# Audio tower on one core: the second normalisation's block turns moved ahead of two expert tiles, bo's third addition moved, gate products on 317 columns

## The chip, the core and the metric

The kernel runs on one core of a Trainium2 chip. The core has five engines with queues of their own: TensorE (PE, with its weight loads shown as PEld), VectorE (DVE), ScalarE (ACT), GpSimd (POOL) and SyncE (SP), which here only issues DMAs. Each engine executes its instructions in the order in which the program gives them, and waits on semaphores for the others. The metric is the device time of one execution in microseconds (us); lower is better.

## What is computed

A batch of 64 signals of 80000 samples is cut into 157 frames of 512 samples each. A DCT of the frames is the embedding `h`. Then follow one attention-like layer and one mixture-of-experts layer, each on a normalised input and added to `h`. The reference, cut to what matters:

```python
h = einsum('bfh,kh->bfk', frames, D)                  # 64 x 157 x 512

x = layernorm(h)                                      # attention
key, qry = exp(1j*pi*tanh(x@Wk+bk)), exp(1j*pi*tanh(x@Wq+bq))
V = x @ Wv + bv
total = sum over 4 sets s of w[s] * Re( cumsum(key_s * V) * conj(qry_s) )
gate = sigmoid(x @ Wg + bg)
total = gate*total + (1-gate)*sigmoid(pos_weight)*retrieved_pos
h = h + x + (total / norm) @ Wo + bo

x = layernorm(h)                                      # experts
scores = softmax(mean(x, axis=1) @ Wg2 + bg2)         # one expert of 16 for each signal
idx = argmax(scores)
h = h + max(scores) * (x @ We[idx] + be[idx])
```

All data is float32.

## The kernel before

**Tiles.** Signals are worked on in 16 groups of 4 (`g` = 0 to 15). A group's tokens lie in five tiles of 128: tiles 0 to 3 hold 32 tokens of each of the 4 signals, and the tail tile (`TAIL`) holds the last 29 of each, filled up to 32. Where the tokens are columns (`xT`, `gT`), the order of the tiles is 0, 1, TAIL, 2, 3, and the 640 columns are two halves of `HN` = 320: the first half is tile 0, tile 1 and signals 0 and 1 of the tail, the second half is signals 2 and 3 of the tail and tiles 2 and 3. So the last 3 columns of the first half (`Q - LT` = 32 - 29) belong to no token.

**Products by seven.** The three large products of a group (values, gate, output) are each done as a 2 x 2 block product with seven block products instead of eight. `product` (line 445) does one for values and output, `gate_product` (line 655) for the gate. Some of their operands are sums of blocks, made by `token_sums`: `new(0)`, `new(2)` on the engine it is given, then `new(1)` and `new(3)` on DVE (line 99), one at each `next(made)`. `new(1)` is used by product 6, `new(3)` by product 3, the last one. `gather` adds a product from PSUM into the results. In the gate, products 4 and 7 take the second half of the columns, products 1, 2, 3, 5 and 6 the first half or sums over both halves, and all have 320 columns. PSUM holds four tiles of two banks (`psum()`), taken in turn by whatever TensorE computes next.

**Stages of a group.** The whole schedule is written by hand: in the order of the program each engine gets its queue. For g from 1 to 15:

1. `project_and_values(g)`: the projection to phases (TensorE, line 600; tanh on ACT), then the value products and the value of the tail. Between them stands work for the second normalisation of the group before: `turn_blocks(g - 1, n)` turns 32 x 32 blocks of the normalised tile n on DVE (line 785) into `blocks2`; `normal2(g - 1, 0)` and `normal2(g - 1, 1)` normalise tiles 0 and 1 on ACT (line 776). When all five tiles are turned, `move_blocks` sends them as 16 DMAs, ten from SP's queue and six from POOL's, to `x2T`, and `xsum`, `route_own`, `route_all` (a small matmul, line 840) and `pick` choose the experts; `fetch` has their weights brought by four indirect DMAs from POOL (4 MB). `keep_value` and `keep_product` (which calls `gather`) bring values from PSUM to SBUF.
2. `gate(g)`: the seven gate products, and between them the scores (line 681), `pick_gate`, `bias` (an indirect DMA for be) and the embedding of group g + 1 with its statistics.
3. `experts_and_embedding(g)`: the expert tiles TAIL, 0 and 1 of group g - 1, and for group g + 1 the normalisation of the residual (`embed_res`, ACT, line 323).
4. `attention(g)`: `add_bo` (POOL, line 327) adds bo to the residual tiles of group g + 1. `read(g, c)` for c = 0 to 3 is the reading of the attention (TensorE, line 697); its result is multiplied into `gT` by DVE (line 704), and a second part added by POOL for c = 0 and 1 (line 708, from a copy `rest` that ACT makes, line 707), by DVE for c = 2 and 3. Then come the seven output products in the order 1, 2, 6, 7, 5, 4, 3, with `statistics2` (means and deviations of the second normalisation, DVE lines 232 and 233, then POOL lines 237 to 244) for TAIL after the first and for tiles 2 and 3 at product 4. After the products come the expert tiles 2 and 3 of group g - 1, the statistics of tiles 0 and 1, `value_sums(g + 1)` (the first two token sums of the next group's values, on POOL), and `normal2` of tiles 2 and 3.

**What stands in whose queue.** `expert(g, n)` is 32 matmuls (64 records in the trace for two tiles), then `expert_out`: DVE multiplies the PSUM tile by the gate and adds it to the residual (line 956), and four DMAs store the tile, from SP. In the program of before, DVE's statistics of tiles 0 and 1 stand behind the two outputs of expert tiles 2 and 3, the five turns behind these, some of them behind the second sum of the values. `blocks2` lies in the same buffer as `gT`, one after the other, and the normalised tiles `x2` in the buffers of the values `v`.

Lines that the change and the prediction's steps touch: 392 `alike`, 399 `token_sums`, 455 `gather`, 647 `gate_product`, 1090 `project_and_values`, 1173 `value_sums`, 1180 `attention`.

Of the kernel before, what the change touches and what calls it, by code (L numbers as in the profile page):

```python
# [28 lines left out]
Q = P // GB  # L29
NM = LP // Q  # L30
TAIL = NM - 1
SLOT = [0, 1, 3, 4, 2]
HT = P // 2
HN = HT + 2 * P
LT = L - Q * TAIL
# [18 lines left out]
def audio_tower(ctx: ExitStack, tc: tile.TileContext, a, out):  # L54
# [21 lines left out]
    nc = tc.nc  # L76
# [14 lines left out]
    def psum():  # L91

        return ps_mm.tile([P, 2, 512], F32, tag="mm", name="mm")
# [6 lines left out]
    add = lambda *x: nc.vector.tensor_tensor(*x, ALU.add)  # L100
# [287 lines left out]
    def halves(x):  # L388

        return [[half(x, m)[:, 2 * k : 2 * k + 2] for k in range(2)] for m in range(2)]  # L390

    def alike(first, second):

        n = 2 * P
        yield first[:, :, :n], second[:, :, -n:]
        if first.shape[2] > n:
            yield first[:, :, n:], second[:, :, :-n]

    def token_sums(g, tail=True, engine=nc.vector):

# [20 lines left out]
    def operand(g, i):  # L421

        (a11, a12), (a21, a22) = S[g]["blocks"]
        return {1: a11, 2: a12, 4: a22}[i] if i in (1, 2, 4) else S[g]["sums"][{3: 3, 5: 0, 6: 1, 7: 2}[i]]
# [3 lines left out]
    def room(g, i):  # L428

        held = S[g].setdefault("held", {})  # L430
        first = i not in ONTO
        ps = psum() if first else held.pop(ONTO[i])
        if i in ONTO.values():
            held[i] = ps
        return ps, first
# [19 lines left out]
    def gather(i, ps, c):  # L455

        (c11, c12), (c21, c22) = c  # L460
        if i == 1:
            nc.scalar.copy(c12, ps)
        elif i == 2:
            nc.scalar.copy(c11, ps)  # L464
        elif i in (4, 7):
            for (x, y), (_, to) in zip(alike(c12, ps), alike(c12, c21 if i == 4 else c22)):
                add(to, x, y)
        elif i == 5:
            for x, to in alike(ps, c22):
                add(to, x, to)  # L470
        else:
            add(c12, ps, c12)


    def value_buffer(g, n):
# [113 lines left out]
    def by_halves(ps):  # L589

        return ps[:, :, :HN]
# [18 lines left out]
    def fold_phases(g):  # L610
        u = S[g]["u"]
        nc.vector.scalar_tensor_tensor(u[:, 1], u[:, 0], -1.0, u[:, 0], ALU.mult, ALU.max)
# [34 lines left out]
    def gate_product(g, i):  # L647

        s = S[g]
        if i == 1:  # L650
            s["gT"] = p1.tile([P, C, 2 * HN], F32, tag="gT", name="gT")
        (ps, first), rhs, w = room(g, i), operand(g, i), fac_g[i]
        for o in range(2):
            for c in range(2):
                nc.tensor.matmul(  # L655
                    ps[:, o, :HN],
                    w[:, c, o * P : (o + 1) * P],
                    rhs[:, c],
                    start=(first and c == 0),
                    stop=(c == 1),  # L660
                    skip_group_check=not first,
                )
        part = halves(s["gT"])
        if i != 2:
            gather(i, by_halves(ps), part)
        for k, m, n in ((2, 0, 0), (5, 1, 1), (3, 0, 1), (4, 1, 0)):
            if k == i:
                for o in range(2):
                    to = part[m][n][:, o]
                    c = 2 * n + o  # L670
                    of = ps[:, o, :HN] if i == 2 else to
                    nc.scalar.activation(to, of, AF.Tanh, bias=hbg[:, c : c + 1], scale=0.5)  # L672

    def scores(g):
# [85 lines left out]
    def at_end(g, n):  # L760

        return g + 1 == NG and n in (3, 0, 1)

    def normal2(g, n):
        s = S[g]
        if n == TAIL:
            x = p1.tile([P, D], F32, tag="v_t", name="x2_t")
        else:
            if n % 2 == 0:
                s["x22"] = p1.tile([P, 2, D], F32, tag="v", name="x2", bufs=2)  # L770
            x = s["x22"][:, n % 2, :]
        rstd, shift = s.pop(("st2", n))
        if at_end(g, n):
            nc.vector.tensor_scalar(x, s["res"][n], shift, rstd, ALU.subtract, ALU.mult)
        else:
            nc.scalar.activation(x, s["res"][n], AF.Identity, bias=shift, scale=rstd)  # L776
        s["x2", n] = x

    def turn_blocks(g, n):

        s = S[g]
        if n == TAIL:
            s["blocks2"] = p1.tile([P, C * GB, LP], F32, tag="gT", name="turned2")
        to = s["blocks2"].rearrange("p (q c) t -> p c q t", c=C)[..., Q * n : Q * (n + 1)]
        nc.vector.transpose(to, s.pop(("x2", n)).rearrange("p (c q t) -> p c q t", c=C, q=GB))
# [155 lines left out]
    def expert_chunk(g, n, c, ps):  # L941

        s = S[g]
        for i in range(GB):
            nc.tensor.matmul(  # L945
                ps[Q * i : Q * (i + 1), :],
                s["x2T"][:, c, i, Q * n : Q * (n + 1)],
                s["ws"][i][:, c, :],
                start=(c == 0),
                stop=(c == C - 1),  # L950
            )
# [13 lines left out]
    def expert(g, n, between=lambda c: None):  # L965
        ps = psum()
        for c in range(C):
            between(c)
            expert_chunk(g, n, c, ps[:, 0, :])
        between(C)  # L970
        expert_out(g, n, ps[:, 0, :])
# [118 lines left out]
    def project_and_values(g):  # L1090

        project(g)
        made = S[g].pop("made")
        turn_blocks(g - 1, TAIL)
        turn_blocks(g - 1, 2)
        fold_phases(g)
        turn_blocks(g - 1, 3)
        value_product(g, 1)
        keep_product(g)
        normal2(g - 1, 0)  # L1100
        normal2(g - 1, 1)
        value(g, TAIL)
        next(made)
        if g == 1:
            for n in (2, 3, TAIL):
                add_bo(g, n)
        turn_blocks(g - 1, 0)
        keep_value(g, TAIL)
        turn_blocks(g - 1, 1)
        moves = move_blocks(g - 1)  # L1110
        next(moves)
        S[g - 1]["late"] = xsum(g - 1, 2 * Q, L)
        value_product(g, 2)
        keep_product(g)
        add_bv(g, 0, slice(0, H))
        next(moves)
        phasors(g)
        value_product(g, 6)
        keep_product(g)
        route(g - 1)  # L1120
        value_product(g, 7)
        keep_product(g)
        route_own(g - 1)
        value_product(g, 5)
        keep_product(g)
        next(made)
        fold_once(g + 1, 0)
        value_product(g, 4)
        keep_product(g)
        route_all(g - 1)  # L1130
        pick(g - 1)
        fetch(g - 1)
        value_product(g, 3)
        keep_product(g)
        weigh()
        fold_twice(g + 1, 0)
# [36 lines left out]
    def value_sums(g):  # L1173

        S[g]["blocks"] = halves(S[g]["xT"])
        S[g]["made"] = made = token_sums(g, engine=nc.gpsimd)
        next(made)
        next(made)

    def attention(g):  # L1180
        ahead = g + 1 < NG
        if ahead and g > 0:
            for n in (0, 1):
                add_bo(g + 1, n)
        if g == 0:
            for _ in weight_sums(wg, t_g, nc.gpsimd):
                pass
        for c in range(C):
            read(g, c)
            if ahead and g > 0:  # L1190
                for n in ((2,), (3, TAIL), (), ())[c]:
                    add_bo(g + 1, n)
        S[g]["blocks"] = halves(S[g]["gT"])
        made = token_sums(g, tail=False)
        if g == 0:
            for n in (0, 1):
                add_bo(1, n)
        for i in (1, 2, 6, 7, 5, 4, 3):
            output_product(g, i)
            if i == 1:  # L1200
                for _ in range(4 if g else 3):
                    next(made)
                if g == 0:
                    scale_all(1)
                output_tail(g)
                statistics2(g, (TAIL,))
            elif i == 6:
                normal2(g, TAIL)
            elif i == 7 and g == 0:
                next(made)  # L1210
            elif i == 5 and g == 0:
                value_sums(1)
            elif i == 5 and ahead:
                scale_all(g + 1)
        if 0 < g and ahead:
            expert(g - 1, 2)
            expert(g - 1, 3)
        for of in ((0, 1),) if ahead else ((0,), (1,)):
            statistics2(g, of)
        if 0 < g and ahead:  # L1220
            value_sums(g + 1)
        normal2(g, 2)
        normal2(g, 3)
        if not ahead:
            normal2(g, 0)

    for g in range(NG):
        if g == 0:
# [12 lines left out]
    g = NG - 1  # L1241
# [158 lines left out]
```

## Time and profile before

| | us |
|---|---|
| median of 3 runs | 1310.64 (1310.27 to 1313.44) |
| the profiled execution | 1311.08 |
| its span, first to last instruction | 1309.1 |
| start to the first projection (group 0) | 45.8 |
| group 0 | 49.1 |
| groups 1 and 2 | 79.2 and 79.3 |
| groups 3 to 14 together | 952.3 (79.36 each) |
| group 15 and the end | 103.4 |

A group is counted here from the first matmul of its projection (line 600) to that of the next. One of the middle groups, from 412.15 to 491.50, has this busy time of the engines by stage, in us:

| stage | from:to | length | PE | DVE | ACT | POOL |
|---|---|---|---|---|---|---|
| projection and values | 412.15:430.45 | 18.30 | 18.30 | 16.37 | 8.61 | 10.88 |
| gate and embedding | 430.45:451.25 | 20.80 | 20.80 | 16.37 | 8.52 | 10.50 |
| experts TAIL, 0, 1 | 451.25:461.68 | 10.43 | 10.43 | 9.05 | 3.24 | 4.62 |
| reading | 461.68:468.81 | 7.13 | 7.13 | 4.10 | 3.50 | 5.68 |
| output products | 468.81:484.61 | 15.80 | 15.80 | 14.07 | 1.40 | 4.18 |
| experts 2, 3 | 484.61:491.50 | 6.89 | 6.89 | 3.71 | 1.52 | 1.43 |

A float32 matmul leaves two records in the trace. A record's length is from its start to its modelled end, and records overlap, so that the distance of two starts, not the length, is what a matmul takes of TensorE. Where a matmul or a weight load waits, the wait lies before its start, or within the record if the weights come late.

### The profile page before, as it was taken

The page shows a single profiled execution, that of the slowest core. Times are in us where ns is not written, and L with a number is a line of the kernel's source. Part 1 is how long each engine was busy: PE and PEld are TensorE (multiplying, and loading weights), DVE is VectorE, ACT ScalarE, POOL GpSimd, SP SyncE. Part 2 cuts the span into 40 slices and gives each one's busy share as a digit, 9 for nine tenths or more (in the row PEclk, how much of TensorE's full clock was granted, in tenths as well). Part 3 has the DMA queues.
Part 4 walks back from the last instruction along what each step waited for, and adds up shares of the span by engine and source line. Part 5 has one row for each costly group of instructions (what it writes and reads, how often), then busy time and mean ns, then how long its engine had stood idle before and what let it go on. Part 6 is the DMA issues. An engine that isn't in the chain of part 4 may idle for free.

```text
span 1309.1 us, 25859 instructions
## 1 busy us (share of the span) xinstructions
PE 1302.9 (100%) x10040; PEld 863.6 (66%) x10040; DVE 1026.9 (78%) x2056; ACT 432.5 (33%) x768; POOL 603.1 (46%) x766
## 2 busy tenths in 40 slices
PE   9999999999999999999999999999999999999998
PEld 6677666676666667666676666766666676666762
DVE  5888787788878878788787877888778787877673
ACT  2524334142432324334143331424323243341410
POOL 2356445344553446435364453446434364343424
PEclk9999999999999999999999999999999999999999
DMA  7015224152341425324252241523314252241506
GB/s 240 1 52 177 75 61 184 41 177 75 111 151 34 168 79 169 95 57 147 82 178 75 68 179 38 178 75 123 135 45 161 82 178 83 57 151 37 179 9 209
DMA packets 60578, 144.45 MB, mean 110 GB/s; under 512 B 14136, under 2 KB 31432, under 8 KB 52520
## 3 DMA queue, kind: packets, MB, share of 16 engines
q1 hardware_dynamic: 45620, 62.68, 16.9%
q0 software_dynamic: 14336, 79.47, 16.7%
q8 instruction: 80, 1.31, 0.4%
q10 hardware_dynamic: 500, 0.64, 0.2%
q14 instruction: 42, 0.34, 0.1%
HBM read 102.47 MB, written 20.62 MB: 94 GB/s over the span
## 4 chain that ended last, share of the span: by engine, by line
PE 98%; POOL 1%; DMA 1%; issue 0%; DVE 0%; POOLq 0%
PE mm L445 29%; PE mm L945 20%; PE mm L655 18%; PE mm L250 9%; PE mm L697 9%; PE mm L270 3%; PE mm L272 3%; PE mm L600 3%; PE mm L636 1%; PE mm L681 1%; PE mm L201 1%; DMA t_v<-in_we,rows 1%; PE mm L219 0%; PE mm L191 0%; PE mm L840 0%
## 5 line engine op out<-in xcount | busy, mean ns | idle before, releaser
L945 PE MATMUL mm<-we,x2T 128*32 128x512 f32 x2400 | 264.1, 593 | 0.0
L945 PEld LDWEIGHTS mm<-we,x2T 128*32 128x32 f32 x2400 | 74.8, 110 | 167.3 <-issue 165.5
L237 POOL TENSOR_SCALAR rstd<-mv 128x2 f32<-128x2 f32 (+1 forms) x50 | 11.8, 236 | 292.6 <-DVE mv L233 292.5
L697 PE MATMUL mm<-att,v 32*128 32x320 f32 (+3 forms) x2048 | 113.1, 357 | 0.0
L697 PEld LDWEIGHTS mm<-att,v 32*128 32x128 f32 x2048 | 94.5, 185 | 22.1 <-issue 12.6
L956 DVE SCALAR_TENSOR_TENSOR res<-mm,gate,res 128x512 f32<-128x512 f32 x64 | 47.9, 749 | 73.1 <-PE mm L945 73.1
L237 POOL TENSOR_SCALAR dev<-mv 128x5 f32<-128x5 f32 (+1 forms) x20 | 10.5, 525 | 196.8 <-DVE mv L233 196.2
L776 ACT ACTIVATE x<-res,shift,rstd 128x512 f32<-128x512 f32 x61 | 46.4, 806 | 162.6 <-POOL shift L244 161.4
L704 DVE TENSOR_TENSOR gT<-mm,gT 128x320 f32<-128x320 f32 x128 | 59.5, 484 | 42.6 <-PE mm L697 42.5
L100 DVE TENSOR_TENSOR gT<-mm,gT 128x320 f32<-128x320 f32 (+3 forms) x128 | 71.4, 567 | 23.9 <-PE mm L655 20.9
L232 DVE BATCH_NORM_STATS2 st<-res 128x6 f32<-128x512 f32 x128 | 87.7, 685 | 2.8
L327 POOL TENSOR_TENSOR res<-res,bo 128x512 f32<-128x512 f32 x64 | 81.6, 1288 | 13.1 <-ACT res L323 13.0
L445 PE MATMUL mm<-t_o,sum 128*128 128x256 f32 x384 | 85.5, 379 | 0.0
L515 POOL TENSOR_TENSOR v<-v,bv 128x512 f32<-128x512 f32 (+1 forms) x45 | 72.7, 1635 | 24.5 <-ACT v L464 24.4
L672 ACT ACTIVATE gT<-gT,hbg 128x320 f32<-128x320 f32 x90 | 45.6, 554 | 112.8 <-DVE gT L100 112.8
L323 ACT ACTIVATE res<-res,shift,more 128x512 f32<-128x512 f32 x64 | 46.9, 803 | 103.7 <-POOL more L313 103.7
L445 PE MATMUL mm<-t_v,sum 128*128 128x256 f32 x360 | 80.1, 379 | 0.0
L445 PEld LDWEIGHTS mm<-t_o,sum 128*128 128x128 f32 x384 | 73.0, 190 | 9.9
L899 POOL DMA_INDIRECT we<-in_we,rows x60 | 60.4, 1006 | 34.3 <-DVE rows L895 20.3
L445 PEld LDWEIGHTS mm<-t_v,sum 128*128 128x128 f32 x360 | 68.4, 190 | 9.3
L250 PE MATMUL mm<-wv,xT 128*128 128x512 f32 x160 | 71.8, 592 | 0.0
L655 PE MATMUL mm<-xT,wg 128*128 128x320 f32 x240 | 69.5, 432 | 0.0
(220 smaller groups left out, 2877.9 us busy)
## 6 DMA issues: line engine op xcount, KB each, us to landing
xT<-in_frames SPq DMA_DIRECT2D x32, 640.0 KB
out<-res SPq DMA_DIRECT2D x236, 64.0 KB
x2T<-turned SPq DMA_DIRECT2D x150, 80.0 KB
x2T<-turned POOLq DMA_DIRECT2D x90, 80.0 KB
scale<-row SPq DMA_DIRECT2D x15, 320.0 KB
out<-res_t SPq DMA_DIRECT2D x62, 32.0 KB
out<-res_t SPq DMA_DIRECT2D x62, 26.0 KB
wg<-in_wg SPq DMA_DIRECT2D x1, 1024.0 KB
```

The source lines that it names most:

```text
L100: add = lambda *x: nc.vector.tensor_tensor(*x, ALU.add)
L232: nc.vector.bn_stats(st, h)
L250: nc.tensor.matmul(ps, tile_of(x[:, c], n), w[:, c, :], start=(c == 0), stop=(c == C - 1))
L327: nc.gpsimd.tensor_tensor(r, r, bo, ALU.add)
L445: nc.tensor.matmul(ps[:, b, :], lhs[:, c, P * b : P * (b + 1)], w[:, c, :], start=(first and c == 0), stop=(c == 1), skip_group_check=not ...
L515: nc.gpsimd.tensor_tensor(v, v, by, ALU.add)
L655: nc.tensor.matmul(ps[:, o, :HN], w[:, c, o * P : (o + 1) * P], rhs[:, c], start=(first and c == 0), stop=(c == 1), skip_group_check=not f ...
L697: nc.tensor.matmul(to, s["v", n][q, c * P : (c + 1) * P], by, start=(n == 3), stop=(n == TAIL))
L704: nc.vector.tensor_tensor(th, r[:, :, 0], th, ALU.mult)
L899: nc.gpsimd.indirect_dma_start(out=ws[b][:, n * k : n * (k + 1)], out_offset=None, in_=of, in_offset=bass.IndirectOffsetOnAxis(ap=rows[:, ...
L945: nc.tensor.matmul(ps[Q * i : Q * (i + 1), :], s["x2T"][:, c, i, Q * n : Q * (n + 1)], s["ws"][i][:, c, :], start=(c == 0), stop=(c == C - 1),
L956: nc.vector.scalar_tensor_tensor(o, ps, s["gate"], o, ALU.mult, ALU.add)
```

## The change

1. **Gate products on 317 columns.** Products 1, 2, 3, 5 and 6 of the gate run over 317 columns instead of 320, and the results that they alone make are read and written on 317 columns. Since products 4 and 7 still read all 320 columns of one result, its last 3 columns are set to zero by a memset on POOL when the tile is made.
2. **End of `attention(g)` for g = 1 to 14.** The expert tiles 2 and 3 of group g - 1 go behind the statistics of tiles 0 and 1, the normalisations of tiles 2, 3, 0 and 1, `value_sums(g + 1)` and the turns of TAIL, 2 and 3. The turns of tiles 0 and 1 stand between the two expert tiles. On TensorE nothing changes its place.
3. **`project_and_values(g)` for g = 2 to 15.** The turns and normalisations of the group before are no longer there. The second `next(made)`, the sum `new(3)`, goes from behind `keep_product` of product 5 to before `keep_value` of the tail.
4. **bo.** For g = 1 to 14 `add_bo` of tile 2 stands before the reading and not behind `read(g, 0)`.

For g = 1 the first stage is left as it was.

```diff
@@ gather @@
+        tight = lambda x: x[:, :, : ps.shape[2]]
         if i == 1:
-            nc.scalar.copy(c12, ps)
+            nc.scalar.copy(tight(c12), ps)
...
         else:
-            add(c12, ps, c12)
+            add(tight(c12), ps, tight(c12))
@@ gate_product @@
         if i == 1:
             s["gT"] = p1.tile([P, C, 2 * HN], F32, tag="gT", name="gT")
+            nc.gpsimd.memset(s["gT"][:, :, HN - (Q - LT) : HN], 0.0)
         (ps, first), rhs, w = room(g, i), operand(g, i), fac_g[i]
+        width = HN if i in (4, 7) else HN - (Q - LT)
         for o in range(2):
             for c in range(2):
                 nc.tensor.matmul(
-                    ps[:, o, :HN],
+                    ps[:, o, :width],
                     w[:, c, o * P : (o + 1) * P],
-                    rhs[:, c],
+                    rhs[:, c, :width],
...
@@ project_and_values @@
         project(g)
         made = S[g].pop("made")
-        turn_blocks(g - 1, TAIL)
-        turn_blocks(g - 1, 2)
+        if g == 1:
+            turn_blocks(0, TAIL)
+            turn_blocks(0, 2)
         fold_phases(g)
-        turn_blocks(g - 1, 3)
+        if g == 1:
+            turn_blocks(0, 3)
         value_product(g, 1)
         keep_product(g)
-        normal2(g - 1, 0)
-        normal2(g - 1, 1)
+        if g == 1:
+            normal2(0, 0)
+            normal2(0, 1)
         value(g, TAIL)
         next(made)
         if g == 1:
             for n in (2, 3, TAIL):
                 add_bo(g, n)
-        turn_blocks(g - 1, 0)
+            turn_blocks(0, 0)
+        else:
+            next(made)
         keep_value(g, TAIL)
-        turn_blocks(g - 1, 1)
+        if g == 1:
+            turn_blocks(0, 1)
         moves = move_blocks(g - 1)
...
         value_product(g, 5)
         keep_product(g)
-        next(made)
+        if g == 1:
+            next(made)
@@ attention @@
         if ahead and g > 0:
-            for n in (0, 1):
+            for n in (0, 1, 2):
                 add_bo(g + 1, n)
...
             read(g, c)
             if ahead and g > 0:
-                for n in ((2,), (3, TAIL), (), ())[c]:
+                for n in ((), (3, TAIL), (), ())[c]:
                     add_bo(g + 1, n)
...
-        if 0 < g and ahead:
-            expert(g - 1, 2)
-            expert(g - 1, 3)
         for of in ((0, 1),) if ahead else ((0,), (1,)):
             statistics2(g, of)
-        if 0 < g and ahead:
-            value_sums(g + 1)
         normal2(g, 2)
         normal2(g, 3)
         if not ahead:
             normal2(g, 0)
+        elif g > 0:
+            normal2(g, 0)
+            normal2(g, 1)
+            value_sums(g + 1)
+            for n in (TAIL, 2, 3):
+                turn_blocks(g, n)
+            expert(g - 1, 2)
+            for n in (0, 1):
+                turn_blocks(g, n)
+            expert(g - 1, 3)
```

`alike`, which pairs the columns of two halves, gets an end for its last piece that also holds where the two differ in width.

More of the change, by code (lines that the diff above doesn't have):

```diff
@@ L396, in alike @@
         if first.shape[2] > n:
-            yield first[:, :, n:], second[:, :, :-n]
+            yield first[:, :, n:], second[:, :, : first.shape[2] - n]
     def token_sums(g, tail=True, engine=nc.vector):
@@ L664, in gate_product @@
         if i != 2:
-            gather(i, by_halves(ps), part)
+            gather(i, ps[:, :, :width], part)
         for k, m, n in ((2, 0, 0), (5, 1, 1), (3, 0, 1), (4, 1, 0)):
@@ L670, in gate_product @@
                     c = 2 * n + o
-                    of = ps[:, o, :HN] if i == 2 else to
+                    to = to[:, :width] if m == 0 else to
+                    of = ps[:, o, :width] if i == 2 else to
                     nc.scalar.activation(to, of, AF.Tanh, bias=hbg[:, c : c + 1], scale=0.5)
```

## The prediction

> **What bounds the kernel now.** I read the busy shares and the chain of waits first. Columns of part 1: engine, busy us, share of the span, instructions.
>
> ```profile
> span 1309.1 us, 25859 instructions
> PE 1302.9 (100%) x10040; PEld 863.6 (66%) x10040; DVE 1026.9 (78%) x2056; ACT 432.5 (33%) x768; POOL 603.1 (46%) x766
> ...
> PE 98%; POOL 1%; DMA 1%; issue 0%; DVE 0%; POOLq 0%
> ```
>
> TensorE is busy for all but 6.2 us and is 98% of the chain. So work moved between DVE, ACT and POOL is worth only the TensorE waits that go with it. The busy share hides short waits, because a matmul that waits for its weights counts as busy. I looked for them in the starts on the timeline. A middle group repeats exactly: the projection (L600) starts at 412.15 and at 491.50, 79.35 us apart. In that period I found two places where TensorE waits for something that the change touches. The first, on the timeline (start, length, engine, line, count):
>
> ```profile
> 427.15 0.68 DVE L100 TENSOR_TENSOR v<-mm,v 128x512 f32<-128x512 f32 x1
> 427.75 0.81 DVE L99 TENSOR_TENSOR sum<-xT,sum 128x640 f32<-128x640 f32 x1
> ...
> 428.10 0.41 PEld L840 LDWEIGHTS mm<-own,mean 128*128 128x128 f32 x2
> 428.32 0.33 PE L840 MATMUL mm<-own,mean 128*128 128x64 f32 x2
> ...
> 428.62 0.51 PEld L445 LDWEIGHTS mm<-wv,sum 128*128 128x128 f32 x3
> 428.62 0.70 PE L445 MATMUL mm<-wv,sum 128*128 128x256 f32 x2
> ```
>
> DVE ends the fourth sum (L99) at 428.56, and the weights of value product 3, which are that sum, load at 428.62. TensorE stood for it. The two first matmuls cover 0.70 us where two undisturbed ones (216 ns apart, 379 ns long) cover 0.60: 0.10 us of the wait sits inside a busy record. The second place is at the start of the output products; the last bracket is idle time and its releaser:
>
> ```profile
> 466.35 1.28 POOL L327 TENSOR_TENSOR res<-res,bo 128x512 f32<-128x512 f32 x1
> ...
> 467.58 1.70 POOL L708 TENSOR_TENSOR gT<-gT,rest 128x320 f32<-128x320 f32 x2
> ...
> 469.33 1.16 PEld L445 LDWEIGHTS mm<-wo,gT 128*128 128x128 f32 x6 [0.22 <-POOL gT L708]
> ...
> PEld mm L445 <- POOL gT L708: 3.2, 14, 0.2
> ```
>
> POOL's third bo addition delays its two gT additions of c = 1 to 469.28, and output product 1 needs them. The last line, from the list of waits, says that this happens in 14 groups. Last, the place into which most is moved, around the two expert tiles (64 matmul records from 405.26):
>
> ```profile
> 407.67 0.66 DVE L100 TENSOR_TENSOR res<-mm,res 128x512 f32<-128x512 f32 x1
> ...
> 408.97 0.75 DVE L956 SCALAR_TENSOR_TENSOR res<-mm,gate,res 128x512 f32<-128x512 f32 x1 [0.65 <-PE mm L945]
> ...
> 412.41 0.75 DVE L956 SCALAR_TENSOR_TENSOR res<-mm,gate,res 128x512 f32<-128x512 f32 x1 [2.68 <-PE mm L945]
> ```
>
> DVE idles 3.3 us here for the tiles' outputs, with the statistics queued behind.
>
> **What the Trainium skill says.** "TensorE: Matmul & The Clock Gate", LDWEIGHTS: a load takes its columns over 1.2 GHz, an estimate of 107 ns for 128; two loads that nothing hides stand 0.11 us apart here (428.62 and 428.73), which agrees. The same page, Back-to-back issue gap: N/2.4 + 2.5 ns. The trace differs in the slope: eight 320-column records go from 430.45 to 432.61, 270 ns each, so 0.83 ns per column and record, with two records per float32 matmul. "GPSIMD Engine Reference", Specifications: GpSimd shares VectorE's SBUF interfaces and contends with instructions that have two SBUF inputs. It agrees: the second sum (L99) takes 1.88 us beside POOL's, the fourth, with the same shape, 0.81 us.
>
> **Gate without filling columns.** Five of the seven gate products lose 3 of 320 columns: 5 x 4 matmuls x 2 records x 3 x 0.83 ns = 0.10 us, in 15 groups 1.5 us, all on TensorE. If odd widths are rounded up inside it is 0. DVE and ACT save less than 1% of operations that nobody waits for. The small memset of gT on POOL stands between the expert fetches and be's fetch (437.28). POOL's first memsets show its price: 0.10 us for 128x5. It waits for the last readers of the old tile in that buffer, the block moves, and the DMA share is 0 from 430 on. Behind it be's fetch, a fold and the bv additions run until 443.3, and POOL's next work begins at 455.87. If that cover were gone it would be 0.10 x 15 = 1.5 us; I take 0.
>
> **The fourth sum.** In groups 2 to 15 it moves from behind value product 5 to ahead of keeping the tail value, so it ends near 418 and not at 428.56. Product 3 then waits only for keeping product 5 (427.15 + 0.68 = 427.83), which is before it is its turn. Gain: the loads then follow the one at 428.32 by 0.11 us, to 428.43, so product 3 has weights at 428.54 instead of 428.73: 0.19 us. At most the whole 0.19 + 0.10 us. If another wait is hidden behind it, 0. Taken: 14 x 0.19 = 2.6 us (0 to 4.1).
>
> **bo's third addition.** POOL has done two bo additions by 463.27. A third ends by 464.5, before the first rest is there (464.64), so c = 0 is not delayed. It leaves the place at 466.35, and the c = 1 additions run when their input is ready (466.44) and end near 468.2, before the product's first weights load (468.81). The load at 469.33 is then prefetched; the interval before the next matmul falls from 305 to 216 ns: 14 x 0.09 = 1.2 us. If the first load too was waiting in part (its transition costs 0.05 us more than the others') it is 1.9; if c = 0 were delayed, 0.
>
> **Statistics, normalisations, turns.** Nothing is added: groups 2 to 15 execute the same two statistics, four normalisations and five turns earlier. From 408.33 DVE does the statistics in 1.7 us (their length now), to 410.0; then three turns (0.6 to 0.7 each), to about 412.0, whose last input ACT has at 411.05. The first expert output then ends at 412.8 and not 409.7. POOL needs 1.9 us for the shift (414.85 to 416.71 now), so 412.0; ACT normalises tiles 0 and 1 by 413.6; their turns end at about 414.3; the second output at 415.1 instead of 413.2. Queued behind are SP's stores of the two tiles, 3.1 and 1.9 us later, whose buffers are wanted only in the next gate stage, and the two PSUM tiles. Of four, the first is next taken by the tail value (416.25), the second by value product 6 (421.41): 3.4 and 6.3 us spare. POOL's two sums run from 412.0 to about 416.0 instead of 416.68 to 420.57; DVE's second sum ends by 417.4 even at 1.88 us, wanted at 421.41. Then SP's ten block moves go at 415 instead of 422; POOL's six stay where they are, behind bv, which waits for value product 2. The fetch follows by about 1 us at most; its traffic ends before 448 now and is used at 451.25. All this is off the path: 0. What it does for the path is to leave DVE 3 to 5 us less to do in the value products, cover for the fourth sum.
>
> **Sum.** 1.5 + 2.6 + 1.2 = 5.3 us, with ends of 0 and 7.5. The profiled execution took 1311.08 us (span 1309.1, 2.0 around it): 1305.8. It lies 0.44 above the median shown, 1310.64, so that the median becomes 1305.3. What is late next in a group are the fixed pauses of about 0.1 us where TensorE changes its tile shape; these stay.
>
> **Rivals.**
> Only the columns and bo: product 3's wait is taken over by the next link (keeping product 5 or the route's own matmul). For it: DVE has no gap between 418.38 and 428. Against: 3 to 5 us of its work leave just that stretch, and keeping product 5 ends 0.5 us before it is wanted. Gain 2.7: 1307.9.
> The change doesn't do what it says: the columns are rounded, c = 0 of the reading is held up by the third addition and loses what c = 1 gains. The margin at 464.64 is only 0.1 us. Gain below 1: 1310.
> Slower: a PSUM tile stays taken. The first expert output now stands behind turns that wait for ACT, which waits for POOL's shift. Should that chain or POOL's sums beside DVE's turns hold it beyond 416.25, TensorE stops at the tail value in 14 groups. It decides from 3.4 us of delay on; 1 us beyond it costs 14, less 5.3: 1319.3. Against: turns beside POOL's sums take 0.70 us now, as without.
>
> **Numbers.** Forecast 0.70, only columns and bo 0.14, nothing moves 0.07, slower 0.09. A measurement of this kernel can tell 0.3%, 3.9 us, from no change: faster needs 1306.7 or less. The forecast's own range (gains of 4 to 7.5, 1303.1 to 1306.7) lies just beyond it. I put faster at 0.70, same at 0.21, slower at 0.09. The range takes in the second case: 1303.3 to 1308.8.
>
> **What would show it.** Right: a period near 79.0 us in groups 2 to 14; the load of product 3's weights 0.11 us behind the route's; no wait of PEld for POOL gT; gate records at 267 ns for five products; expert outputs near 412 and 414.5. Wrong: any gap on TensorE at the tail value or product 6, a wait of ACT for the memset at gate product 1, or bo's additions ending after the first rest.

## The result and the profile after

The changed kernel takes 1305.9 us, median of 6 runs (1304.4 to 1307.56), beside 1311.57 us for the kernel before, median of 6 runs (1310.27 to 1313.44). The ratio is 0.996, with a 95% interval of 0.9949 to 0.997: faster by 0.43%, 5.7 us. The prediction was 1305.3 us.

The page of the changed kernel, its span, busy times and chain of waits:

```profile
span 1302.5 us, 25848 instructions
PE 1295.9 (99%) x10040; PEld 861.8 (66%) x10040; DVE 1010.2 (78%) x2056; ACT 432.2 (33%) x768; POOL 594.7 (46%) x781
...
PE 98%; DMA 1%; POOL 1%; issue 0%; SPq 0%; DVE 0%; POOLq 0%
```

TensorE still bounds the kernel, with the same 10040 records. DVE and POOL lost 17 and 8 us of busy time, although POOL got 15 instructions more; how that comes about is seen below. The page can't tell where 5.7 us went, so I took the starts of the projection in each group from the timelines. The stretches of this table, with the thirteen groups 2 to 14, add up to the span:

| stretch, us | before | after |
|---|---|---|
| start, up to group 0's projection | 45.77 | 45.54 |
| group 0 | 49.14 | 49.14 |
| group 1 | 79.19 | 79.00 |
| each of groups 2 to 14 | 79.36 | 78.98 |
| group 15 and the end | 103.39 | 102.11 |

The start, whose program is the same in all kernels profiled here, took 45.4 to 48.1 us in them; the end took 102.1 to 103.3 us in the variants of the changed kernel below (105.2 in run 7). So the 1.3 us by which the end is shorter, of the 6.6 us between the two spans, say little. The 13 middle groups are the reliable part: 0.38 us each (79.357 less 78.978 on average), 4.9 us.

Within a group, two waits of TensorE went. The timeline of the changed kernel around the route's matmuls (start, length, engine, line, operation, count):

```profile
425.46 0.68 DVE L100 TENSOR_TENSOR v<-mm,v 128x512 f32<-128x512 f32 x1
...
426.57 0.41 PEld L844 LDWEIGHTS mm<-own,mean 128*128 128x128 f32 x2
426.78 0.33 PE L844 MATMUL mm<-own,mean 128*128 128x64 f32 x2
426.89 1.60 PEld L445 LDWEIGHTS mm<-wv,sum 128*128 128x128 f32 x8
426.95 1.95 PE L445 MATMUL mm<-wv,sum 128*128 128x256 f32 x8
```

Product 3 now starts 0.17 us after the first of the route's matmuls, where it was 0.30 us before, and its eight weight loads form one unbroken row. From start to start of single records, the step from the route to product 3 fell from 246 to 112 ns and the next from 320 to 271 ns, together 0.183 us in this group, 0.188 on average of the 13. On DVE, keeping product 5 (L100) ends at 426.14, well ahead. The timeline of the changed kernel at the output products:

```profile
463.71 2.66 POOL L712 TENSOR_TENSOR gT<-gT,rest 128x320 f32<-128x320 f32 x3
466.33 1.27 POOL L327 TENSOR_TENSOR res<-res,bo 128x512 f32<-128x512 f32 x1
466.98 1.59 PEld L445 LDWEIGHTS mm<-wo,gT 128*128 128x128 f32 x8
```

POOL has finished its additions into gT at 466.37, ahead of its next bo addition and 0.6 us before the weight loads of output product 1, all eight of which stand in one row. The interval in it that was 305 ns is 216 ns. The list of PEld's waits has no line with POOL gT any more. The first additions into gT aren't late either: the third bo addition ends at 462.72, and POOL then waits 0.17 us for ACT's copy `rest`. Third, the list of groups by form:

```profile
L658 PE MATMUL mm<-xT,wg 128*128 128x317 f32 x240 | 68.9, 430 | 0.0
...
L653 POOL MEMSET gT<- 128x12 f32 x15 | 1.9, 125 | 0.0
```

The busy mean of such a record says little, since matmuls overlap. From start to start, records of 317 columns are 267 ns apart and those of 320 columns 269 ns. The memset costs POOL 1.9 us in all, and no other engine waits for it.

Last, the place into which the statistics, normalisations and turns were moved, on DVE's timeline (the bracket is idle time and its releaser):

```profile
408.44 0.68 DVE L789 STREAM_TRANSPOSE turned<-x_t 128x512 f32<-128x512 f32 x1
409.05 1.26 DVE L789 STREAM_TRANSPOSE turned<-x 128x512 f32<-128x512 f32 x2
410.23 0.71 DVE L960 SCALAR_TENSOR_TENSOR res<-mm,gate,res 128x512 f32<-128x512 f32 x1
411.12 1.42 DVE L789 STREAM_TRANSPOSE turned<-x 128x512 f32<-128x512 f32 x2 [0.18 <-ACT x L780]
412.46 0.71 DVE L960 SCALAR_TENSOR_TENSOR res<-mm,gate,res 128x512 f32<-128x512 f32 x1
413.99 0.82 DVE L99 TENSOR_TENSOR sum<-sum,xT 128x640 f32<-128x640 f32 x1
414.84 0.82 DVE L99 TENSOR_TENSOR sum<-xT,sum 128x640 f32<-128x640 f32 x1
418.35 0.69 DVE L100 TENSOR_TENSOR v_t<-mm,bv 128x512 f32<-128x512 f32 x1 [2.68 <-PE mm L250]
```

The idle time in which DVE used to wait for the two tiles is filled. In return DVE now stands idle for 2.68 us before it keeps the tail value: it waits for TensorE, where it used to run behind it. The second sum takes 0.82 us; in the kernel before it was

```profile
418.38 1.88 DVE L99 TENSOR_TENSOR sum<-sum,xT 128x640 f32<-128x640 f32 x1 [1.43 <-POOL sum L411]
```

Two things changed for it. DVE had stood idle for 1.43 us ahead of it, waiting for POOL's sums of the values, which stood behind the statistics of tiles 0 and 1; now POOL's sums end at 413.57, before it starts at 413.99. And it ran beside POOL's later sum (L414), which itself took 2.26 us and now takes 1.70. In 14 groups these two shorter sums are 15 of DVE's 17 us and nearly all of POOL's 8 us. That both are slower beside each other agrees with what the Trainium skill says under "GPSIMD Engine Reference", Specifications, on GpSimd's contention with VectorE instructions that have two SBUF inputs; the page gives no size, and here it is a factor of 2.3 for DVE.

### The profile page after: what moved, and what is told of

Its sections match the earlier page's. It is cut to its first block, busy times and chain, and to the rows that moved or that the text cites. A ratio compares the mean times of both kernels' runs of the same rounds, so it can differ in the third digit from the quotient of the medians.

```text
span 1302.5 us, 25848 instructions
## 1 busy us (share of the span) xinstructions
PE 1295.9 (99%) x10040; PEld 861.8 (66%) x10040; DVE 1010.2 (78%) x2056; ACT 432.2 (33%) x768; POOL 594.7 (46%) x781
## 4 chain that ended last, share of the span: by engine, by line
PE 98%; DMA 1%; POOL 1%; issue 0%; SPq 0%; DVE 0%; POOLq 0%
PE mm L445 29%; PE mm L949 20%; PE mm L658 17%; PE mm L250 9%; PE mm L701 9%; PE mm L270 3%; PE mm L272 3%; PE mm L601 3%; PE mm L637 1%; PE mm L685 1%; PE mm L201 1%; DMA t_v<-in_we,rows 0%; DMA wv<-in_wv 0%; PE mm L219 0%; PE mm L844 0%
## 5 line engine op out<-in xcount | busy, mean ns | idle before, releaser
L100 DVE TENSOR_TENSOR gT<-mm,gT 128x320 f32<-128x320 f32 (+3 forms) x128 | 71.2, 566 | 27.4 <-PE mm L658 24.4
L676 ACT ACTIVATE gT<-gT,hbg 128x320 f32<-128x320 f32 (+1 forms) x90 | 45.6, 554 | 116.3 <-DVE gT L100 116.3
L658 PE MATMUL mm<-sum,wg 128*128 128x320 f32 (+1 forms) x240 | 69.2, 431 | 0.0
L658 PE MATMUL mm<-xT,wg 128*128 128x317 f32 x240 | 68.9, 430 | 0.0
```

Of the source, the lines that this page charges most:

```text
L658: nc.tensor.matmul(ps[:, o, :width], w[:, c, o * P : (o + 1) * P], rhs[:, c, :width], start=(first and c == 0), stop=(c == 1), skip_group_ ...
```

## The experiments

The sum of the prediction is close to the measurement. But its terms could still be wrong: the fourth sum's place and the move were changed together, and either could have removed the wait of product 3. Two theories:

- **Place**, as the prediction had it: the fourth sum stood too late in DVE's queue; its earlier place is worth 0.19 us a group and the move nothing by itself.
- **Load**: DVE was late as a whole in the value products. The move unloads it, and with that the wait goes wherever the sum stands.

Where no interval is given, the time is a single run, beside 1310 to 1311 us for the kernel before. The period of the middle groups, which repeats within 0.02 us in a run (one group of run 8 apart), is the finer measure; periods are means of groups 2 to 14.

**1. The change with the fourth sum back behind keeping product 5.**

```diff
@@ project_and_values @@
-        else:
-            next(made)
         keep_value(g, TAIL)
...
         keep_product(g)
-        if g == 1:
-            next(made)
+        next(made)
         fold_once(g + 1, 0)
```

> The changed kernel with the fourth sum of the values back behind keeping product 5, everything else as changed. Theory 'load': what made TensorE wait was that DVE was behind in this stage, and moving statistics and turns out of it is what cures it; then the sum starts behind keeping product 5 (426.06 in the changed kernel's clock), ends at 426.87, and the next weight load could not begin before 426.89 anyway: period 78.98 to 79.00 us as with the change, total within 0.3 us of it. Theory 'place' (the prediction's wording): the sum's place in DVE's queue is what counts; then the wait of 0.18 us per group is back: period 79.16, total 2.6 us longer than the changed kernel.

1305.91 us, median of 4 runs, ratio to the kernel before 0.994 to 0.9973; the period is 79.005 us. The timeline of this kernel at the route:

```profile
426.09 0.68 DVE L100 TENSOR_TENSOR v<-mm,v 128x512 f32<-128x512 f32 x1
426.69 0.81 DVE L99 TENSOR_TENSOR sum<-xT,sum 128x640 f32<-128x640 f32 x1
...
427.41 0.33 PE L844 MATMUL mm<-own,mean 128*128 128x64 f32 x2
427.58 1.97 PE L445 MATMUL mm<-wv,sum 128*128 128x256 f32 x8
```

The sum is again the last thing before product 3, yet product 3 follows the route by 0.17 us: the sum ends at 427.50, when the route's matmuls have just started. In the kernel before it ended 0.24 us after that start (428.56 against 428.32). The next interval is 300 ns on average and not 272. So with the move made, the sum's own place is worth 0.03 us a group. Load holds.

**2. The kernel before with nothing but the fourth sum earlier.**

```diff
@@ project_and_values @@
+        if g > 1:
+            next(made)
         turn_blocks(g - 1, 0)
         keep_value(g, TAIL)
...
         keep_product(g)
-        next(made)
+        if g == 1:
+            next(made)
         fold_once(g + 1, 0)
```

> The kernel before with one thing changed: the fourth sum ahead of keeping the tail value in groups 2 to 15. Theory 'load': DVE has no gap there, the sum's 0.81 us pushes all that follows back, keeping product 5 then ends at about 428.6 where the sum ended at 428.56, and product 3 waits for that instead: period 79.36 as before (79.3 to 79.4). Theory 'place': the wait goes: period 79.17.

1315.56 us beside 1310.65: slower, and neither theory's number. The period is 79.71 us, 0.36 above the kernel before. The timelines of this kernel, DVE and TensorE:

```profile
419.14 1.87 DVE L99 TENSOR_TENSOR sum<-sum,xT 128x640 f32<-128x640 f32 x1 [1.45 <-POOL sum L411]
421.05 0.96 DVE L99 TENSOR_TENSOR sum<-xT,sum 128x640 f32<-128x640 f32 x1
...
427.06 0.67 DVE L100 TENSOR_TENSOR v<-v,mm 128x512 f32<-128x512 f32 x1
...
427.78 1.99 PE L445 MATMUL mm<-t_v,xT 128*128 128x256 f32 x8 [0.28 <-DVE v L100]
...
429.61 0.33 PE L840 MATMUL mm<-own,mean 128*128 128x64 f32 x2
429.78 1.51 PE L445 MATMUL mm<-wv,sum 128*128 128x256 f32 x6
```

Product 3 again follows the route by 0.17 us; its wait is gone. But product 4, which adds onto the PSUM tile of product 7, now waits until DVE has kept product 7, at 427.73. Its first two intervals are 657 ns on average and 320, where two undisturbed ones are 216 each: 0.54 us lost, 0.18 won, 0.36 in all. The kernel before had just 0.6 us to spare there: this line of its DVE timeline

```profile
425.30 0.67 DVE L100 TENSOR_TENSOR v<-v,mm 128x512 f32<-128x512 f32 x1
```

ends at 425.97, and its product 4 starts at 426.59. A 0.8 us sum put in front uses that up. Both theories as I had put them fall here: from the second sum on DVE's queue was full, and the sum only moved the delay to the next one who waits. That is the mechanism of the prediction's rival "only the columns and bo", though at product 4 and not at product 3, and only without the move.

**3. The move alone.** The statistics, normalisations, turns and `value_sums` are those of the change; the fourth sum, bo's third addition and the 320 columns are those of before.

```diff
@@ gate_product @@
-            nc.gpsimd.memset(s["gT"][:, :, HN - (Q - LT) : HN], 0.0)
...
-        width = HN if i in (4, 7) else HN - (Q - LT)
+        width = HN
@@ project_and_values @@
-        else:
-            next(made)
...
-        if g == 1:
-            next(made)
+        next(made)
@@ attention @@
-            for n in (0, 1, 2):
+            for n in (0, 1):
...
-                for n in ((), (3, TAIL), (), ())[c]:
+                for n in ((2,), (3, TAIL), (), ())[c]:
```

> Only the move: statistics, normalisations, sums on POOL and turns ahead of and between the two expert tiles, with the fourth sum, bo's third addition and the gate's 320 columns as before. Theory 'load': the wait for the fourth sum goes with the move alone: period 79.17 (79.355 less 0.18), total 2.6 us less than before. Theory 'place': the wait stays, period 79.36, total as before.

1308.48 us, median of 11 runs, beside 1310.53 us, ratio 0.998 (0.9971 to 0.9989). The period is 79.19 us, 0.17 below the kernel before. The timeline of this kernel at the route:

```profile
428.64 0.68 DVE L100 TENSOR_TENSOR v<-mm,v 128x512 f32<-128x512 f32 x1
429.24 0.81 DVE L99 TENSOR_TENSOR sum<-xT,sum 128x640 f32<-128x640 f32 x1
...
429.96 0.33 PE L843 MATMUL mm<-own,mean 128*128 128x64 f32 x2
430.13 1.97 PE L445 MATMUL mm<-wv,sum 128*128 128x256 f32 x8
```

The sum is where it was in the program and ends, at 430.05, close enough behind the route's start that product 3 follows by 0.17 us; 0.03 us of the wait stay in the next interval, as in run 1. The move removes the rest. It has two parts that no run here separates: DVE's statistics and turns are done earlier, and so are POOL's sums, for which DVE had idled 1.43 us and beside which its second sum took 1.06 us longer. Against the route's start the fourth sum ended only 0.15 us later before than here (0.24 and 0.09 us behind it), so by these figures either part alone may be enough.

**4 and 5. The change without one small part each.** First with all gate products on 320 columns and without the memset:

```diff
@@ gate_product @@
-            nc.gpsimd.memset(s["gT"][:, :, HN - (Q - LT) : HN], 0.0)
...
-        width = HN if i in (4, 7) else HN - (Q - LT)
+        width = HN
```

> The changed kernel with all gate products on 320 columns again and without the memset. If the width counts as 0.83 ns per column and record, 40 records of 3 columns: period 79.08 (+0.10). If an odd width is rounded up or the memset costs as much: 78.98.

1307.44 us, period 79.08: 0.10 us a group for the columns, so 0.83 ns for each of the 3 columns of 40 records. The odd width of 317 is not rounded up. Then with bo's third addition back behind the first reading:

```diff
@@ attention @@
-            for n in (0, 1, 2):
+            for n in (0, 1):
...
-                for n in ((), (3, TAIL), (), ())[c]:
+                for n in ((2,), (3, TAIL), (), ())[c]:
```

> The changed kernel with bo's third addition back behind the first reading. If POOL's queue is what the output product waited for: the interval of 305 ns is back in 13 full middle groups, period 79.07 (+0.09). If something else of the change freed it: 78.98.

1306.81 us, period 79.066: 0.09 us a group.

With runs 1 to 5 the account of a middle group is closed: columns 0.100, bo 0.088, the move 0.169, the fourth sum's place after the move 0.028, together 0.385 us beside 0.379 measured.

**6 to 8. How much later may the expert outputs come?** The prediction's slower case put the limit at 3.4 us, at a PSUM tile that the tail value takes next. These three repeat the turn of TAIL ahead of the first expert output, with the same input and the same output, so that only DVE's queue grows:

```diff
@@ turn_blocks @@
-    def turn_blocks(g, n):
+    def turn_blocks(g, n, times=1):
...
-        nc.vector.transpose(to, s.pop(("x2", n)).rearrange("p (c q t) -> p c q t", c=C, q=GB))
+        x = s.pop(("x2", n)).rearrange("p (c q t) -> p c q t", c=C, q=GB)
+        for _ in range(times):
+            nc.vector.transpose(to, x)
@@ attention @@
             for n in (TAIL, 2, 3):
-                turn_blocks(g, n)
+                turn_blocks(g, n, 6 if n == TAIL else 1)
```

That is five repeats; the others have 11 and 9 in place of 6.

> The changed kernel with the turn of the tail tile done five times more, the same data to the same place, ahead of the first expert output in groups 1 to 14: at a pitch of 0.61 us it delays that output by 3.05 us, so that it ends at 414.0 where the tail value takes its PSUM tile at 414.71. If PSUM is the only thing that waits for DVE here: period 78.98, nothing lost. If something else waits for the turns or outputs, the period grows by up to 3 us.

1307.53 us, period 78.98: nothing lost. A repeat costs 0.745 us, so the delay was 3.7 us. The first expert output ends at 417.14 in this kernel and the tail value starts at 417.18, so this run stays just inside the limit of the prediction; the next two go beyond it.

> The same with ten times more: delay 6.1 us, the first expert output ends at about 417.0, 2.3 us after the tail value wants its PSUM tile. If the slower case of the prediction is right in its mechanism and its point: TensorE stops at the tail value, period 81.2 to 81.6, total 32 to 36 us longer. If PSUM tiles are not the limit: less than 79.5.

1349.28 us, period 82.20, so 3.2 us lost with a delay of 7.45 us. TensorE's timeline in this kernel, in another group:

```profile
342.07 3.60 PE L250 MATMUL mm<-wv,xT 128*128 128x512 f32 x8
345.85 1.99 PE L445 MATMUL mm<-wv,xT 128*128 128x256 f32 x8 [0.18 <-ACT v L463]
348.78 5.45 PE L445 MATMUL mm<-t_v,sum 128*128 128x256 f32 x24 [0.94 <-DVE sum L99]
355.12 1.99 PE L445 MATMUL mm<-t_v,xT 128*128 128x256 f32 x8 [0.89 <-DVE v L100]
```

The tail value starts on time at 342.07, although the first expert output leaves its PSUM tile only at 345.75. So the tile that I had named isn't the one that it takes. TensorE stops at product 2, which adds onto the PSUM tile of product 1, because ACT's copy of product 1 (L463) comes late; on ACT's timeline that copy is

```profile
345.21 0.59 ACT L463 COPY v<-mm 128x512 f32<-128x512 f32 x1 [4.30 <-DVE turned L791]
```

It waits for a turn, since the normalised tiles and the values share a set of buffers. By the intervals this costs 0.44 us. Larger are the stops at product 6, for DVE's second sum (1.21 us), and at product 4, for keeping product 7 (1.16). A fourth, at gate product 7, costs 0.41 us.

> Eight more turns of the tail tile, at the pitch of 0.745 us that ten of them showed: 5.96 us of delay. Theory 'PSUM tile at the tail value' (3.4 us spare): TensorE stops there for over 2 us, period above 81. Theory 'shared buffer and queue': the first stop is ACT's copy of product 1, which waits for the turn of tile 3 because normalised tiles and values share buffers; with ten more that was late by 0.34 us, with eight it is in time, and only the second sum and keeping product 7 in DVE's queue come up to 0.5 us late: period 79.0 to 79.8.

1315.86 us, period 79.78: 0.8 us lost with a delay of 5.96 us. There is no stop at the tail value or at product 2. Products 6 and 4 lose 0.17 and 0.21 us to DVE's queue. The rest is a single stop of 0.41 us at gate product 7, the one that run 7 has too. Its releaser is ACT's activation of the gate (L676). That instruction starts 7.50 us after the gate stage does, here as in the changed kernel, where product 7 starts without waiting for its end; and the stop is just as long in run 7, with 1.5 us more delay. So a late DVE doesn't explain it, and why TensorE waits there in these two kernels stays open. The move's reserve thus lies between 3.7 and 6 us; then DVE's queue decides (0.38 us at 5.96), and only above that, between 6 and 7.5 us, do the shared buffers come in.

**9. All five turns ahead of both expert tiles.**

```diff
@@ attention @@
-            for n in (TAIL, 2, 3):
+            for n in (TAIL, 2, 3, 0, 1):
                 turn_blocks(g, n)
             expert(g - 1, 2)
-            for n in (0, 1):
-                turn_blocks(g, n)
             expert(g - 1, 3)
```

> The changed kernel with all five turns ahead of both expert outputs. The first output then ends at about 412.5 and nothing of TensorE's wants it for microseconds: period 78.98. If the split, two turns between the expert tiles, is what keeps TensorE running: longer by the lateness of the first output.

1307.43 us, period 78.98: the same. Putting the last two turns between the expert tiles is not needed. None of the nine has a shorter period than the changed kernel.

## Why the prediction was right, and where it was not

The total was right: 5.3 us predicted, 5.7 measured. The stretches of the profile account for 5.4 us: 4.9 in the middle groups, 0.2 in group 1, 0.3 in group 15. By the prediction's steps:

- **Columns**, 0.10 us a group: right, shown by run 4. The width of 317 isn't rounded up, and the memset (0.125 us each, 0.10 expected) is hidden.
- **bo's third addition**, 0.09: right, shown by run 5. The feared delay of c = 0 didn't come: POOL has 0.17 us to spare there.
- **The wait of product 3**, 0.19 us: the size was right (0.188 us in the intervals). Its owner was not. The prediction booked it under "the fourth sum" and gave the move 0, as mere cover. The runs show the reverse: the move alone brings 0.17 us a group, 13 x 0.17 = 2.2 us in the middle groups, and the sum's place 0.03 us after it. Without the move the sum's place costs 0.36 us a group, since the prediction overlooked that keeping product 7, with 0.6 us to spare, stands behind the new place of the sum. That this term came out right was luck: the change made both moves at once. The prediction saw the symptom (the named releaser of the wait) and not the state: a queue that is late from the second sum on. POOL's earlier sums it counted as off the path too, though DVE waited 1.43 us for them. A hint lay in the trace before: in group 1 the intervals at the route were 111 and 272 ns although the sum stood in its old place. There no expert outputs stand in DVE's queue, POOL's sums end at 95.24, soon after the projection starts, and DVE even waits 0.56 us for TensorE before it keeps product 6.
- **Order of the moved work**: right. The first expert output was predicted to end at 412.8 on the clock of the profile before. The group starts 1.53 us earlier in the profile after, so that is 411.3 there; it ended at 410.94. The second was predicted at 415.1, thus 413.6, and ended at 413.17. DVE's second sum was allowed up to 1.88 us and took 0.82.
- **The slower rival** did not come, as the prediction held, but its mechanism was wrong: runs 7 and 8, with delays well above its 3.4 us, show no stop at the tail value. The first margin to run out is that of DVE's queue.

What stays open is the end of the kernel, 1.28 us shorter in the profile. The columns and product 3's wait in group 15 explain some 0.28 us of it (0.10 and 0.18). The remaining 1 us lies in the last group's expert tiles, for whose weights TensorE waits on DMA, and is no more than the end varies by between the profiles (102.1 to 103.3 us).

## What to carry to other kernels

When an engine is 99% busy, look at start-to-start intervals for the rest: a matmul that waits for its weights hides the wait in a busy record. The releaser named at a wait may be only the last in a queue that is late as a whole; ask how much each consumer of that queue has to spare before moving one item ahead, because the item pushes all others back by its length. Here unloading the queue into its idle time elsewhere cured the wait, and moving the item alone did harm. Ask also what the late queue itself waits for: here it was in part another engine's work. A reserve that was worked out from buffers can be tested by repeating an instruction whose result stays the same, and the first limit may be another than the one worked out.

## What was not expected of the hardware

- A transpose of 128x512 repeated with the same input and output follows the one before by 0.745 us, while turns of different tiles follow by 0.61 (408.44 to 409.05). A delay made by repetition was thus longer than the spacing of the kernel's own turns suggested.
- Float32 records of 64 columns that follow each other with a weight load each (L219 at the start of the changed kernel) start 112 ns apart, and so do their loads. It isn't the columns that set this: at the rate of the 320-column records (269 ns) 64 columns would be 54 ns, and the route's two records, whose loads are 216 ns apart and early, do start 55 ns apart. The 112 ns agree with the estimate of 107 ns for a load that follows from the Trainium skill, "TensorE: Matmul & The Clock Gate", LDWEIGHTS.
- The list of PEld's waits of the changed kernel has a new line:

```profile
PEld mm L445 <- issue: 15.3, 63, 0.5
PEld mm L445 <- DVE turned L789: 7.3, 14, 0.5
```

It looks like a new wait of 0.5 us in 14 groups. The intervals at that place, from the projection to product 1, are 363 and 320 ns, and they were 363 and 320 before, where the time was booked as issue (22.6 us and 15.3 now). A line that appears in such a list is not yet a loss.
